# Scanning two states in one VectorE instruction, with a start column between them

## The chip, the cores and the metric

One core of a Trainium2 chip runs the whole program. The metric is the device time of one execution in microseconds; the time given for a kernel is the median of several runs. A profile is one further execution, recorded instruction by instruction; its span is the time from the first to the last instruction.

## The reference

Two sequences of 2048 tokens with 256 channels are normalised (layer norm) to `xn`. The result is `x + scan(xn) + experts(xn)`.

The scan part sorts the tokens of each sequence by their nearest of eight means, and runs a selective scan along the sorted order, with 16 states for each channel:

```
delta = softplus(dt_proj(u) + bias)                    # per token and channel
h[n]  = exp(delta * A[n]) * h[n] + (delta * u) * B[n]  # for each of 16 states n
y     = sum over n of h[n] * C[n]  +  D * u
```

The rows `y` are then put back into the tokens' own order. The expert part is a mixture of eight experts (two linear maps up to 512 with a SiLU gate, one down to 256), of which each token takes the best two.

## The kernel before

**Stages.** A front part of some 110 us normalises, scores, sorts and routes the tokens. After it, the scan and the experts run interleaved to the end. The scan is cut into 8 pieces of 512 positions (`CH`), four for each sequence; channels lie on the 128 partitions, in two halves `h`. The expert work is cut into 71 tiles of 128 tokens, each made of two parts up (8 matmuls each as written, which the trace records as 16) and one part down.

**The scan of a piece.** `gather` fetches the rows, `turn` transposes them to `u`, `project` makes delta, B and C, `step_size` and `series` make `dl` (delta, with softplus as a series of squares by ScalarE and multiply-adds by VectorE) and `du` (delta * u). `load_b` brings B of four states, repeated on all partitions, into a tile `bt`; `load_z` and `mask_z` bring C into a block form `z`. Then come steps (`Step`), one for a group `q` of four states and a half `h`: 64 in all. In a step, for each state `i`:

- `decay(i)`: ScalarE computes `da = exp(dl * A)`, 512 columns;
- `feed(i)`: VectorE computes `bu = du * bt[i]`;
- `scan(i)`: VectorE scans `da` and `bu` along the 512 positions, starting from a column of `carry` (or from 0 in a sequence's first piece), and writes every fourth element of `hs`, so that the four states of a position lie together.

`keep_last` copies the last position to `carry` (ScalarE). `turn(i)` (in `Step`) transposes four blocks of `hs` on TensorE into a PSUM tile `pt_s` (two buffers), which ScalarE copies to `ht`; `contract(i)` multiplies `ht` with `z` and sums the states in PSUM (`ys`). At a piece's end `take_sums` copies the sums to `yt` and `add_sums` adds its rows, through GpSimd, to `acc` or, for the last piece, to the output.

**The order.** The order of instructions on each engine is that of the program's text, so the loop at its end decides it. It counts in places: each step has `NSUB` = 4 places, and in place `i` of step `k` it emits the next product, `scan(i)`, `decay(i)` of the step after, and part of the transposes and contractions of the step before (places 1 and 2 turn, place 3 contracts). `at_place(step, place, ...)` puts all other scan work (loads, masks, series, projections, sums) at chosen places. The experts' parts (`jobs`) are given out at a pace: as many as keep the planned TensorE time in a fixed ratio to the planned VectorE time (`on_pe`, `on_dve`); those still left 16 scans before the end are all emitted there. VectorE's work on a part (`silu`, `gate`) is emitted two places after the part's matmuls (`later`). Once all experts' parts are out, the two halves of `acc` are copied to the output, and the last piece's rows are added to that.

**Queues.** `load_b`, `load_z` and the store of the projection go through SP's queue in the order of the text, each waiting there until its tile is free; weight tiles, token rows and row additions go through GpSimd's.

**Buffers.** `bt` two tiles of four states, `da` six tiles of one state, `bu` three, `hs` three tiles of four states, `ht` four, `pt_s` two.

## Time and profile before

| | before |
|---|---|
| median of 3 runs | 800.16 us (799.86 to 808.87) |
| the profiled execution | 793.45 us |
| its span | 791.7 us |
| TensorE busy | 712.9 us (90%) |
| VectorE busy | 711.3 us (90%) |
| ScalarE busy | 507.9 us (64%) |
| GpSimd busy | 520.9 us (66%) |
| mean granted TensorE clock | 0.951 |

How to read it: the shares are of the whole span, and so mix the front part, the interleaved part and the end. The chain of work that ended last runs over TensorE for 69% of the span and over VectorE for 3%. Lines of groups give the line, the engine, the operation, what is written and read, the shapes and the number of instructions, then busy us and mean ns of one, then the idle time just ahead of them. DMA lines give the number of issues, KB each, and the median time from issue to landing. Numbers of lines are those of the kernel before.

### The profile page before, as it was taken

To read this page: it belongs to the slowest core of one execution; us is meant where nothing else is said; L and a number is where in the kernel's file an instruction comes from. 1 tells how busy PE (TensorE), PEld (TensorE's weight loads), DVE (VectorE), ACT (ScalarE), POOL (GpSimd) and SP (SyncE) were. 2 spreads that over 40 slices of the span, in tenths; PEclk is the share of its full clock that TensorE was granted. 3 is DMA by queue.
4 is the path that set the end of the run, shared out by engine and by line. 5 is a ranking of instruction groups with operands and counts; after the bars stand their busy time and mean duration, and the time that the engine had idled before them with its cause. 6 is when DMAs were issued, how large, how long until landed. Compare 5 with 4: busy or idle time off the path is not lost.

```text
span 791.7 us, 16967 instructions
## 1 busy us (share of the span) xinstructions
PE 712.9 (90%) x6552; PEld 605.5 (76%) x6552; DVE 711.3 (90%) x1162; ACT 507.9 (64%) x986; POOL 520.9 (66%) x374
## 2 busy tenths in 40 slices
PE   7385979899999999899999999999999998999963
PEld 5144768589877988599868986798779885998842
DVE  8865269899999999899989999899999998899991
ACT  4821266586669657776668666866687576757572
POOL 2023738657867886788776787878678787686313
PEclk9755999999999999999999999999999998999996
DMA  8593244664368547855656367448644855444462
GB/s 280 222 323 114 58 173 108 210 172 97 108 155 244 154 106 215 203 148 143 206 140 176 56 247 219 107 95 263 197 111 132 273 156 112 107 102 96 86 219 27
DMA packets 61215, 125.90 MB, mean 159 GB/s; under 512 B 24464, under 2 KB 42032, under 8 KB 53776
## 3 DMA queue, kind: packets, MB, share of 16 engines
q0 software_dynamic: 40224, 65.03, 34.6%
q1 hardware_dynamic: 20912, 59.80, 22.1%
q8 instruction: 52, 0.85, 0.4%
q14 instruction: 27, 0.22, 0.1%
HBM read 180.06 MB, written 27.00 MB: 262 GB/s over the span
## 4 chain that ended last, share of the span: by engine, by line
PE 69%; ACT 6%; DVE 3%; issue 3%; DMA 2%; POOL 1%; POOLq 0%; SPq 0%; ACTq 0%; DVEq 0%
PE p_ps L875 28%; PE py L898 14%; PE pt_s L787 12%; PE y L796 6%; ACT ht L791 2%; DMA out_dram<-acc 2%; PE y L728 2%; PE pt_g L858 2%; PE px L655 2%; PE pd L692 1%; DVE hs L775 1%; ACT da L760 1%; DVE bu L766 1%; PE px L660 1%; PE pt_u L641 1%
## 5 line engine op out<-in xcount | busy, mean ns | idle before, releaser
L875 PE MATMUL p_ps<-xT,w 128*128 128x128 f32 x2272 | 280.3, 279 | 5.3 <-ACT sq L702 4.3
L875 PEld LDWEIGHTS p_ps<-xT,w 128*128 128x128 f32 x2272 | 268.2, 195 | 20.2 <-issue 9.3
L775 DVE TENSOR_TENSOR_SCAN hs<-da,carry,bu 128x512 f32<-128x512 f32 x192 | 246.2, 1283 | 0.0
L760 ACT ACTIVATE da<-dl,na 128x512 f32<-128x512 f32 x256 | 182.0, 723 | 1.1 <-DVE hs L775 1.0
L816 POOL DMA_INDIRECT acc<-yo,token_of x71 | 137.8, 1941 | 60.3 <-ACT yo L902 20.0
L766 DVE TENSOR_TENSOR bu<-du,bt 128x512 f32<-128x512 f32 x256 | 174.0, 680 | 0.0
L791 ACT COPY ht<-pt_s 128x512 f32<-128x512 f32 x256 | 137.1, 590 | 31.3 <-PE pt_s L787 31.0
L787 PE MATMUL pt_s<-ident,hs 128*128 128x128 f32 x1024 | 137.9, 279 | 14.7 <-ACT ht L791 8.7
L835 POOL DMA_INDIRECT w<-in_w_up_dram,w_row x71 | 94.8, 1335 | 84.2 <-DVE w_row L584 36.8
L898 PE MATMUL py<-w,g 128*128 128x256 f32 x568 | 139.0, 389 | 12.2 <-ACT r L696 8.7
L787 PEld LDWEIGHTS pt_s<-ident,hs 128*128 128x128 f32 x1024 | 117.7, 143 | 31.6 <-ACT ht L791 15.6
L898 PEld LDWEIGHTS py<-w,g 128*128 128x128 f32 x568 | 104.2, 193 | 27.1 <-ACT r L696 10.3
L849 POOL DMA_INDIRECT xg_sb<-xn,token_of x71 | 88.3, 1243 | 37.5 <-issue 30.2
L835 POOL DMA_INDIRECT w<-in_w_down_dram,w_row x71 | 93.5, 1317 | 21.6 <-issue 12.5
L883 ACT ACTIVATE t_sb<-p_ps 128x512 f32<-128x512 f32 x71 | 42.5, 599 | 69.4 <-PE p_ps L875 69.1
L902 ACT ACTIVATE yo<-py,own 128x256 f32<-128x256 f32 x71 | 33.8, 476 | 80.5 <-PE py L898 80.3
L775 DVE TENSOR_TENSOR_SCAN hs<-da,bu 128x512 f32<-128x512 f32 x64 | 78.2, 1223 | 0.0
L796 PE MATMUL y<-ht,z 128*32 128x128 f32 x2048 | 74.3, 279 | 2.5 <-ACT ht L791 1.9
L816 POOL DMA_INDIRECT acc<-yt,line_of x28 | 54.7, 1952 | 25.7 <-ACT ht L791 8.2
L796 PEld LDWEIGHTS y<-ht,z 128*32 128x32 f32 x2048 | 51.1, 110 | 24.5 <-issue 13.2
L888 DVE SCALAR_TENSOR_TENSOR t_sb<-t_sb,p_ps 128x512 f32<-128x512 f32 x71 | 48.2, 679 | 9.1 <-ACT t_sb L883 8.8
L892 DVE SCALAR_TENSOR_TENSOR g<-t_sb,p_ps 128x512 f32<-128x512 f32 x71 | 48.3, 681 | 7.2 <-PE p_ps L875 4.7
(188 smaller groups left out, 632.8 us busy)
## 6 DMA issues: line engine op xcount, KB each, us to landing
bt<-bc SPq DMA_DIRECT2D x32, 1024.0 KB, 5.4
z<-bc SPq DMA_DIRECT2D x32, 256.0 KB, 3.8
xn<-xt SPq DMA_DIRECT2D x8, 520.0 KB, 2.6
xt<-in_x_dram SPq DMA_DIRECT2D x8, 512.0 KB, 7.5
acc<-in_x_dram SPq DMA_DIRECT2D x8, 512.0 KB, 6.4
w<-in_w_up_dram,w_row POOLq DMA_INDIRECT x71
w<-in_w_down_dram,w_row POOLq DMA_INDIRECT x71
xg_sb<-xn,token_of POOLq DMA_INDIRECT x71
```

The source lines that it names most:

```text
L760: nc.scalar.activation(self.da[i], self.piece.dl[:, self.h, :], AF.Exp, scale=na[:, self.h, n : n + 1])
L766: nc.vector.tensor_mul(self.bu[i], self.piece.du[:, self.h, :], self.piece.bts[self.q][:, i, :])
L775: nc.vector.tensor_tensor_scan(self.hs[:, :, i], self.da[i], self.bu[i], start, ALU.mult, ALU.add)
L787: nc.tensor.transpose(pt[:, j, :], self.hs[:, t0 : t0 + G, :].rearrange("p t n -> p (t n)"), ident)
L791: nc.scalar.copy(self.ht[i], pt)
L796: nc.tensor.matmul(p.ys[self.h][j * G : (j + 1) * G, i, :], lhsT=p.zs[q][:, i * (P // G) + j, :], rhs=self.ht[i][:, j, :], start=False, st ...
L816: ins = nc.gpsimd.indirect_dma_start(out=to, out_offset=bass.IndirectOffsetOnAxis(ap=numbers, axis=0), in_=rows, in_offset=None, compute_o ...
L835: nc.gpsimd.indirect_dma_start(out=to[self.t % NW], out_offset=None, in_=rows, in_offset=bass.IndirectOffsetOnAxis(ap=w_row[:, self.t : se ...
L849: nc.gpsimd.indirect_dma_start(out=self.xg, out_offset=None, in_=xn_d, in_offset=bass.IndirectOffsetOnAxis(ap=token_of[:, self.t : self.t ...
L875: nc.tensor.matmul(p[:, f, :], lhsT=wk[:, h, f * P : (f + 1) * P], rhs=self.xT[:, h, :], start=h == 0, stop=h == ND - 1,)
L892: nc.vector.scalar_tensor_tensor(self.g, self.s, 0.5, self.p3, ALU.mult, ALU.mult)
L898: nc.tensor.matmul(py, lhsT=self.g[:, f, :], rhs=w2[:, f, :], start=f == 0, stop=f == NH - 1)
```

## The change

Two states of a half are now scanned by one VectorE instruction of 1026 columns: 513 for each state. The first column of each state has a decay of 0 and an input that is the state to begin from, so the running value is replaced there. A step covers eight states: four pairs `o`, each made of states `o` and `o + 4` of the eight.

- `bt` becomes `[P, 2, 2, 513]`: it holds two pairs. Each `load_b` issues two DMAs, each for two rows of B that go behind their start columns. A new `begin(i)` lets ScalarE copy four carried states (or zeros) into the start columns of one `bt` tile.
- `du` gets a start column of 1.0 (a memset for each piece), so that the product puts the carried state into `bu`.
- `da` becomes three lasting tiles of two states, with start columns set to 0 once. `decay` still computes one state at a time.
- `feed` and `scan` work on pairs, four of each in a step; the scan starts from 0.0 in all pieces. `hs` has two tiles of eight states.
- A step has eight places: scans in even ones, products in odd ones. Transposes stand in places 1, 2, 4 and 5 of the following step, contractions in 3 and 6.
- `load_b`, `load_z`, `mask_z`, `begin` of the sums, `take_sums` and `add_sums` get other places, in units of four as before. The planned VectorE times are 2.1 and 1.1 us for the two kinds of place.

```diff
         def load_b(self, q: int):
-            bt = scn.tile([P, Q, CH], F32, tag="b", name="bt")
-            nc.sync.dma_start(
-                bt, bc_d[self.b][self.c][q * Q : (q + 1) * Q, :].partition_broadcast(P)
-            )
+            bt = scn.tile([P, 2, 2, CH1], F32, tag="b", name="bt")
+            r0 = q // 2 * 2 * Q + q % 2 * 2
+            for o in range(2):
+                rows = bc_d[self.b][self.c][r0 + o : r0 + o + Q + 1 : Q, :]
+                nc.sync.dma_start(bt[:, o, :, 1:], rows.partition_broadcast(P))
             self.bts[q] = bt
...
-                self.du = prep.tile([P, ND, CH], F32, tag="du", name="du")
+                self.du = prep.tile([P, ND, CH1], F32, tag="du", name="du")
+                nc.vector.memset(self.du[:, :, 0:1], 1.0)
...
+        def begin(self, i: int):
+            p = self.piece
+            nc.scalar.copy(
+                p.bts[2 * self.s + i][:, :, :, 0],
+                carry[:, self.s, self.h, 2 * i : 2 * i + 2, :] if p.c
+                else zero[:, 0:4].rearrange("p (o n) -> p o n", n=2),
+            )
...
-            nc.scalar.activation(
-                self.da[i], self.piece.dl[:, self.h, :], AF.Exp, scale=na[:, self.h, n : n + 1]
-            )
+            nc.scalar.activation(
+                self.da[o][:, n, 1:], self.piece.dl[:, self.h, :], AF.Exp,
+                scale=na[:, self.h, state : state + 1],
+            )
...
+        def feed(self, o: int):
+            self.bu[o] = scn.tile([P, 2, CH1], F32, tag="bu", name="bu", bufs=2)
             nc.vector.tensor_mul(
-                self.bu[i], self.piece.du[:, self.h, :], self.piece.bts[self.q][:, i, :]
+                self.bu[o], self.piece.du[:, self.h, :].unsqueeze(1).to_broadcast([P, 2, CH1]),
+                self.piece.bts[2 * self.s + o // 2][:, o % 2],
             )
...
-                self.hs = late.tile([P, CH, Q], F32, tag="hs", name="hs", bufs=3)
-            start = carry[:, q, h, i : i + 1] if p.c else 0.0
+                self.hs = late.tile([P, 2, CH1, Q], F32, tag="hs", name="hs", bufs=2)
             nc.vector.tensor_tensor_scan(
-                self.hs[:, :, i], self.da[i], self.bu[i], start, ALU.mult, ALU.add
+                self.hs.rearrange("p n t o -> p (n t) o")[:, :, o],
+                self.da[o].rearrange("p n t -> p (n t)"), self.bu[o].rearrange("p n t -> p (n t)"),
+                0.0, ALU.mult, ALU.add,
             )
...
-            at_place(max(s0 + 2 * q - 3, 0), NSUB - 1 if n or q > 1 else 0, lambda p=p, q=q: p.load_b(q))
+        for q, place in ((1, -2), (2, 10), (3, 14)):
+            if n or q > 1:
+                at_place(s0 - 1, NSUB + place, lambda p=p, q=q: p.load_b(q))
...
+        if step:
+            if i % 2 == 0:
+                step.scan(i // 2)
+            elif i // 2 + 1 < Q:
+                step.feed(i // 2 + 1)
+            elif after_:
+                after_.feed(0)
+            if i == 1:
+                step.begin(1)
+            if after_ and i == 5:
+                after_.begin(0)
+            if i + AHEAD < N_STEP:
+                step.decay(i + AHEAD)
+            elif after_:
+                after_.decay(i + AHEAD - N_STEP)
+        if before_:
+            if i == 0:
+                before_.keep_last()
+            elif i in (1, 2, 4, 5):
+                for j in range(2):
+                    before_.turn(i // 4, (i - 1) % 3 * 2 + j)
+            elif i in (3, 6):
+                before_.contract(i // 4)
```

In the piece's count of 32 places, the loads of `bt` for groups 0 to 3 now stand at places -6, -2, 10 and 14 relative to the piece's first scan; `begin` of these tiles for the first half stands at -3, 1, 13 and 17, and the first products from them at -1, 3, 15 and 19.

## The prediction

> **What bounds the kernel now.** I read four views in this order: busy time by stretch, the waits inside the scan loop, the groups of instructions, and the timeline of the last scans. The first says which engines are full. Its columns are the stretch (start:end in us), its length, then busy us and instructions of TensorE, weight load, VectorE, ScalarE and GpSimd, the granted clock, the DMA share and GB/s.
>
> ```profile
> 115.00:200.00 85.00, 80.57 (x731) 70.00 (x731) 81.65 (x133) 55.03 (x110) 58.94 (x42) 1.00 0.50 138
> 200.00:280.00 80.00, 78.42 (x767) 67.42 (x766) 77.98 (x112) 57.56 (x114) 61.73 (x40) 1.00 0.60 164
> 280.00:360.00 80.00, 76.09 (x719) 66.47 (x718) 76.20 (x111) 56.13 (x111) 62.83 (x42) 0.98 0.62 166
> ...
> 746.00:780.00 34.00, 24.15 (x291) 17.37 (x290) 29.63 (x33) 22.19 (x40) 4.05 (x2) 0.90 0.51 159
> ```
>
> From 115 to 746 us TensorE is busy 609.8 of 631 us and VectorE 607.1: idle 21.2 and 23.9 us. Two engines are full at once. From 746 us, when the expert work is over, only VectorE is. Is a "full" TensorE really full? In the timeline around 322 us a run of sixteen p_ps matmuls starts at 321.79 and the next block at 323.57: 111 ns each, and the blocks behind it follow at the same rate without a gap. It works at its own pace; it isn't waiting for data while shown as busy.
>
> Next, who holds whom in that loop (TensorE's waits from 115 to 746 us, us in total, times, longest):
>
> ```profile
> PE py L898 <- ACT r L696: 7.7, 4, 3.1
> PE pt_s L787 <- ACT ht L791: 5.8, 9, 0.9
> ...
> PE p_ps L875 <- DVE g L892: 0.4, 1, 0.4
> ```
>
> TensorE's idle time hangs on ScalarE, which itself waits there almost only for TensorE; VectorE releases 0.4 us of it. The 7.7 us are two pauses of 3.1 us (at 328 and 665 us) and little else: py waits for one of the two buffers of its PSUM pool, which pd holds until ScalarE has made e and r from it behind a decay, a square and a carry; the matmuls right after the pause run at half speed (8 of py in 3.4 us instead of 1.9). So the change takes work from an engine that is full, beside another that is as full and hardly waits for it.
>
> **The change, part by part.** *VectorE's instructions.* Scans go from 256 of 512 columns to 128 of 1026, products likewise. The rows:
>
> ```profile
> L775 DVE TENSOR_TENSOR_SCAN hs<-da,carry,bu 128x512 f32<-128x512 f32 x192 | 246.2, 1283 | 0.0
> L766 DVE TENSOR_TENSOR bu<-du,bt 128x512 f32<-128x512 f32 x256 | 174.0, 680 | 0.0
> L775 DVE TENSOR_TENSOR_SCAN hs<-da,bu 128x512 f32<-128x512 f32 x64 | 78.2, 1223 | 0.0
> ...
> L538 DVE TENSOR_TENSOR_SCAN cum<-keep,both 128x256 f32<-128x256 f32 x1 | 0.7, 693 | 0.0
> ...
> L301 DVE TENSOR_TENSOR fm_c<-sc,bm 128x256 f32<-128x256 f32 x1 | 0.4, 424 | 0.0
> ```
>
> A scan costs (1223 - 693)/256 = 2.07 ns a column, so 1026 columns without a start from a tile cost 1223 + 514 x 2.07 = 2287 ns. A product costs (680 - 424)/256 = 1.0 ns a column: 680 + 514 = 1194 ns. Reading du twice through a stride of 0 is free by a near row: the product with mask, also stretched by such a stride, takes 672 ns for 512 columns. Durations may not simply be added up, as the timeline of the last scans shows:
>
> ```profile
> 760.73 1.28 DVE L775 TENSOR_TENSOR_SCAN hs<-da,carry,bu 128x512 f32<-128x512 f32 x1
> ...
> 761.92 0.67 DVE L766 TENSOR_TENSOR bu<-du,bt 128x512 f32<-128x512 f32 x1
> ...
> 762.51 1.28 DVE L775 TENSOR_TENSOR_SCAN hs<-da,carry,bu 128x512 f32<-128x512 f32 x1
> ```
>
> A scan and a product of 1.95 us together come round every 1.78: each starts 0.09 us before the one ahead ends. Two states cost 3.57 us now (3.45 without a carried start, 60 ns less each), and 2.287 + 1.194 - 0.18 = 3.30 after. The saving is 96 x 0.27 + 32 x 0.15 = 30 us, not the 53 us that the durations alone would give. Eight memsets take back under 1. VectorE in the loop: 607 to about 578 us, 92%.
>
> A rule speaks against this. The Trainium skill (Vector Engine (DVE) Microarchitecture Reference, Measured stream behaviour on trn2) says that pairs of words beginning at an odd word cost 1.30 ns a column on both sources where even ones cost 1.054. With 513 words a row, every second row begins at an odd word; no row of this trace does. By the rule a product could cost up to 1026 x 0.25 = 0.25 us more, 32 us in all, and the saving is gone; by the rows it costs nothing. I take the rows (a long row has one odd start, the rule's case has one at each pair) and keep the rule for a rival.
>
> *ScalarE.* 64 new copies into the column between the states, 24 copies of carry less (48 to 24), at 180 ns (carry copy in the timeline): +7.2 us on 458 of 665; ScalarE idles 172 us of the loop, so the work itself is hidden. Where the cover fails is the wait below.
>
> *A new wait on ScalarE.* Begin writes into bt and must wait until bt has landed; until now only the product on VectorE did. In the new order a load of bt waits for the product in place 9 of a piece's 32 (one place: a scan or a product), SP issues it, ScalarE reaches begin in place 13, and the product needs it in place 15. The other three loads have the same spacing; before, a load came eight places ahead. Behind begin in ScalarE's queue stand a decay, the copies ht of the same place and the experts' copies, and TensorE waits for these. Places last (775.6 - 117.1)/256 = 2.57 us, so the lead to begin is 3.5 x 2.57 = 9.0 us. What does a load take?
>
> ```profile
> bt<-bc SPq DMA_DIRECT2D x32, 1024.0 KB, 5.4
> z<-bc SPq DMA_DIRECT2D x32, 256.0 KB, 3.8
> ...
> bc<-xd SPq DMA_DIRECT2D x8, 64.0 KB, 2.2
> ```
>
> From below: 5.4 us as now, plus 0.33 for a second issue, 5.7. But rows of a partition no longer lie side by side, so pieces shrink from 8 KB to 2 KB. Of such pieces z is made: 3.8 - 2.2 = 1.6 us for 256 KB beyond the smallest transfer, hence 2.2 + 4 x 1.6 = 8.6 us for 1 MB, 8.9 with the issue. z's spread is 2.9 to 7.9 us, bt's 4.3 to 9.6. I take 7 us, between the two, as the queues' own mean (22.1% of 16 x 791.7 us over 20,912 packets, 134 ns each of 2.9 KB) makes 32 packets an engine 4.3 us or less. It fits the lead by 2 us in the median; a late quarter of the 32 loads, some 2 us over and half of that hidden by the two buffers of pt_s, costs about 2 us in all, at worst as in the slower rival. The queue order bears it: SP has the store of xd in front of one load a piece (place 12 before 14), and the loads of z wait for contractions only one place earlier (19 for 20, 22 for 23), with three places and more to the next bt.
>
> *Tiles.* hs has two buffers of eight states instead of three of four. VectorE may write the first buffer again in place 16, TensorE has turned it in place 13, so VectorE can be two to three places ahead; the experts' silu, put two places behind its matmuls, already holds it there. da is six states in both. Costed at 0 with that cover, up to 3 us a step without it. TensorE gets states three places after their last scan, before two: nothing lost.
>
> *TensorE.* Same transposes, contractions and experts: 609.8 us stay.
>
> *Head and tail.* First scan: one wide product instead of a narrow one, +0.5 us. After the last expert's gate 16 scans are left, as before: 8 x 3.30 = 26.4 against 16 x 1.78 = 28.5 us, -2.1. But what follows the last scan doubles: four turns took from 775.8 to 779.0 us, eight take 2.8 us more and a contraction half a microsecond: +3.3. The copy of acc to the output ended at 771.5 and is not what the end waits for. Tail +1.2.
>
> *Sum.* Of TensorE's 21.2 us idle, 6.2 are the two pauses and stay, as step_size keeps its places; of the other 15, held by ScalarE, I let a quarter go because ScalarE's decays and VectorE's gates come earlier: -4. With +2 for late loads, +0.5 and +1.2: about 0, between -4 and +4. Against its own execution of 793.45 us (span 791.7 and 1.75 around it) that is 793 us. The median of the runs, 800.16, lies 0.8% above; scaled, 800 us. As late loads may stay away I say 798.
>
> **The rivals.**
>
> *A. TensorE stays full (forecast).* For: 97% busy, 0.4 us released by VectorE. Against: two engines at 97% cost each other something that no wait names. 792 to 808 us.
>
> *B. The coupling was the price: faster.* With VectorE at 92% TensorE loses nearly all of its 15 us, and the tail gives 2: -17 us, 2.1%, 783 us. For: VectorE idles only 23.9 us, mostly behind ScalarE's squares. Against: the waits.
>
> *C. ScalarE stands before bt: slower.* Loads of 2 KB pieces beside the experts' weights (DMA share 0.6) take z's price and z's doubling, 9 to 16 us, against a lead of 9. It decides from a landing of about 10.5 us, where the two buffers of pt_s no longer hide it. At a mean of 12 us, 3 late and 1 to 1.5 of it seen by TensorE, 32 loads cost 32 to 48 us: 832 to 848; at 10.5 to 11, 816 to 825. For: lead cut to three and a half places. Against: a 1 MB load lands in 5.4 us now.
>
> *D. VectorE does not get quicker.* Odd rows cost the rule's 0.25 us: no saving, tail +3.3 and head +0.5 remain: 803 us, up to 818 if TensorE now waits for scans.
>
> **How the numbers follow.** A 0.40, B 0.15, C 0.35, D 0.10 (0.07 within 2%, 0.03 above). Faster by over 2% 0.15, within 2% 0.47, slower by over 2% 0.38; 2% is about what a measurement of this kernel can tell from no change. The time is A's, 798, with its own range of 788 to 808. The full range cuts B's better half and C's worse third: 783 to 832 us.
>
> **What would show it.** Right: scan rows of 2.29 us and product rows of 1.19, VectorE near 578 us of the loop while TensorE is still at 97%; bt landing in 6 to 8 us; no wait of bt's copy for a DMA over 1 us. Product rows above 1.35 mean D. Waits of bt on ScalarE for bt's DMA, then TensorE on ht, mean C. TensorE idle below 10 us in the loop means B. The forecast is wrong if TensorE's busy time in the loop changes, or if the loop itself is over 12 us longer or shorter.

## The result and the profile after

The changed kernel takes **854.58 us** (median of four runs, 851.05 to 860.40) against 804.28 us for the kernel before (four runs): a ratio of **1.063**, with a 95% interval of 1.053 to 1.073. It is slower by 6%, and lies above the forecast of 798 us and above the whole range of 783 to 832 us. The kernel before was measured anew beside every group of runs below, with medians from 794.86 to 805.5 us; so ratios are compared, not times.

First the groups of the page of the changed kernel: engine totals, then line, engine, operation, shapes, count, busy us and mean ns of one, and the idle time just ahead with what ended most of it.

```profile
PE 732.9 (85%) x6552; PEld 613.6 (71%) x6552; DVE 694.7 (81%) x917; ACT 511.9 (60%) x1026; POOL 577.8 (67%) x374
...
L795 DVE TENSOR_TENSOR_SCAN hs<-da,bu 128x1026 f32<-128x1026 f32 x128 | 293.8, 2295 | 11.9 <-ACT da L780 5.2
...
L787 DVE TENSOR_TENSOR bu<-du,bt 128x1026 f32<-128x1026 f32 x128 | 156.2, 1220 | 19.3 <-ACT bt L767 18.8
...
L860 POOL DMA_INDIRECT w<-in_w_up_dram,w_row x71 | 99.6, 1403 | 80.3 <-DVE w_row L586 36.9
...
L860 POOL DMA_INDIRECT w<-in_w_down_dram,w_row x71 | 115.2, 1622 | 21.6 <-issue 13.7
```

The two instructions of the change last what the prediction gave them (2295 against 2287 ns, 1220 against 1194). VectorE has less to do, 694.7 us instead of 711.3. But look at GpSimd (POOL), which has not one instruction more and was left out of the prediction: 577.8 us instead of 520.9. Its issues of the experts' weights have grown. These are the same rows in the page of the kernel before:

```profile
L835 POOL DMA_INDIRECT w<-in_w_up_dram,w_row x71 | 94.8, 1335 | 84.2 <-DVE w_row L584 36.8
...
L835 POOL DMA_INDIRECT w<-in_w_down_dram,w_row x71 | 93.5, 1317 | 21.6 <-issue 12.5
```

Next the changed kernel's busy time by stretch, with the columns of the table shown in the prediction:

```profile
200.00:280.00 80.00, 74.77 (x718) 63.85 (x720) 72.49 (x77) 54.13 (x112) 61.53 (x37) 1.00 0.62 154
280.00:360.00 80.00, 73.44 (x686) 61.58 (x678) 70.86 (x78) 53.54 (x110) 61.81 (x37) 1.00 0.60 153
...
440.00:520.00 80.00, 68.01 (x642) 59.98 (x640) 65.77 (x74) 48.33 (x98) 63.90 (x39) 0.98 0.53 130
```

Between 200 and 280 us TensorE was busy 78.42 us and VectorE 77.98; now 74.77 and 72.49, with 718 matmul instructions done instead of 767. Both engines that were full have holes, everywhere in the loop. From the first scan to the last expert matmul the loop took 634.1 us before (117.06 to 751.1) and takes 688.7 now (123.51 to 812.2): +54.6 of the +66.8 us of span. The rest is +5.7 behind the last expert matmul and +6.4 ahead of the first scan. The last is not the change's own: the front part is the same, and in other profiles of changed versions the first scan stands anywhere from 115.55 to 123.52 us. The trace of the changed kernel is of the longest of its four executions (860.40 us), and that of the kernel before is of a short one (793.45 us); so these differences are somewhat larger than the 50.3 us between the two medians.

What ended the idle time in the loop (engine, line, what it waited for: us in total, times, longest), 115 to 812 us:

```profile
DVE t_sb L913 <- ACT t_sb L908: 22.9, 19, 5.2
...
DVE bu L787 <- ACT bt L767: 18.8, 9, 8.4
PE pt_s L811 <- ACT ht L815: 18.2, 20, 2.2
...
PE py L923 <- DMA w<-in_w_down_dram,w_row: 13.5, 6, 7.5
```

Two waits of TensorE are new in size: that for `ht` (5.8 us before), and that for the down weights, which the list of before doesn't have. From the first scan to the last expert matmul TensorE idles 63.6 us instead of 21.4. VectorE's wait for `begin` is the one that the prediction feared. Is it because `bt` lands late? No: among ScalarE's waits in this stretch there is none for the DMA of `bt`. The longest of these pauses shows what it hangs on. This is GpSimd's part of the changed kernel's timeline (start, duration, engine, line; in brackets the idle time ahead and what ended it):

```profile
500.43 1.86 POOL L622 DMA_INDIRECT xs<-xn,line_of  x1 [0.30 <-issue]
502.60 1.85 POOL L622 DMA_INDIRECT xs<-xn,line_of  x1 [0.30 <-issue]
504.75 0.95 POOL L622 DMA_INDIRECT xs<-xn,line_of  x1 [0.30 <-issue]
506.00 1.83 POOL L622 DMA_INDIRECT xs<-xn,line_of  x1 [0.30 <-issue]
508.14 1.46 POOL L874 DMA_INDIRECT xg_sb<-xn,token_of  x1 [0.30 <-issue]
509.90 2.73 POOL L841 DMA_INDIRECT acc<-yo,token_of  x1 [0.30 <-ACT da L780]
512.93 1.78 POOL L860 DMA_INDIRECT w<-in_w_down_dram,w_row  x1 [0.30 <-issue]
515.02 2.39 POOL L860 DMA_INDIRECT w<-in_w_up_dram,w_row  x1 [0.31 <-DMA acc<-yo,token_of]
```

And the other engines in the same stretch:

```profile
514.33 2.29 DVE L795 TENSOR_TENSOR_SCAN hs<-da,bu 128x1026 f32<-128x1026 f32 x1
...
522.04 3.33 PE L923 MATMUL py<-w,g 128*128 128x256 f32 x7 [7.53 <-DMA w<-in_w_down_dram,w_row]
...
525.83 0.47 ACT L927 ACTIVATE yo<-py,own 128x256 f32<-128x256 f32 x1 [10.91 <-PE py L923]
526.20 0.19 ACT L767 COPY bt<-zero 128x4 f32<-128x4 f32 x1
...
526.42 1.23 DVE L787 TENSOR_TENSOR bu<-du,bt 128x1026 f32<-128x1026 f32 x1 [8.42 <-ACT bt L767]
```

Read it upwards from the last line. VectorE waits 8.42 us for `begin`. `begin` stands in ScalarE's queue behind `yo`, which waits 10.91 us for `py`. TensorE waits 7.53 us for down weights. They are those issued at 512.93 (the issue ahead of that one stands at 496.96, and the one after it ends 0.1 us before the matmul). It comes at the end of a line of issues with only the queue's own 0.30 us between them: GpSimd is behind with its work.

A long pause of TensorE can cost more than its length. This is the stretch from the end of the pause, with the columns of the table above:

```profile
520.00:526.50 6.50, 4.46 (x13) 3.67 (x14) 0.08 (x1) 0.67 (x3) 3.59 (x4) 0.50 0.96 355
```

The granted clock is 0.50 there, and the seven matmuls of `py` in the line above take 3.33 us. In the loop of the changed kernel the trace has six such stretches of 3.4 or 6.8 us, 30.7 us in all; the kernel before has two, 10.2 us. TensorE's busy time in the loop is 625.1 us instead of 612.6, for much the same matmuls; at half clock the 20.5 us more would account for some 10 of these 12.5 us (an estimate).

And single issues of GpSimd differ: the same `xs` issue takes 0.95 us or 1.85; the `w_up` issue beside the 2.29 us scan takes 2.39 and ends 0.8 us after it.

Sorting GpSimd's issues in the loop by what VectorE runs when they start gives the rule of this trace. In the changed kernel the median `w_up` issue takes 0.99 us (9 cases) beside an idle VectorE and 2.38 us (16 cases) when it starts beside a scan; in the kernel before, where a scan lasts 1.2 to 1.3 us, 0.99 (5) and 1.49 (23). `xg` takes 0.97 (10) and 2.17 us (15), before 0.97 (5) and 1.43 (19). The ends are sharper than the medians: from the first scan on, all 68 issues of weights and `xg` that start beside a scan in the changed kernel end 0.75 to 0.88 us after the end of that scan. (In the kernel before 65 of 79 do; the others start within the first 0.06 or the last 0.15 us of a scan.) It is not a matter of VectorE being busy, as `silu` and `gate` show, of whose two inputs one lies in PSUM (`p_ps`):

```profile
321.81 0.69 DVE L913 SCALAR_TENSOR_TENSOR t_sb<-t_sb,p_ps 128x512 f32<-128x512 f32 x1 [0.69 <-ACT t_sb L908]
...
322.31 1.00 POOL L860 DMA_INDIRECT w<-in_w_up_dram,w_row  x1 [0.30 <-PE pt_s L811]
```

The 37 issues that start beside one of these take 0.97 to 1.07 us, as beside an idle VectorE. So **an issue that starts beside a scan is held until the scan ends, and scans have become twice as long.** The Trainium skill (GPSIMD Engine Reference, 1. Specifications) names a contention that fits: GpSimd shares its SBUF interfaces with VectorE and contends with VectorE instructions that have two SBUF inputs, which scans and products are. It doesn't say that DMA issues are held, nor for how long; these rows do.

Do the transfers themselves take longer as well? For those of GpSimd's queue, no. Its packets took 31.8% of the changed span of 858.5 us and 34.6% of 791.7 us before, which is 273 and 274 us for each of the 16 DMA engines:

```profile
q0 software_dynamic: 40224, 65.03, 31.8%
...
q0 software_dynamic: 40224, 65.03, 34.6%
```

### The profile page after: what moved, and what is told of

It reads as the page before. It is cut to its first block, busy times and chain, and to the rows that moved or that the text cites. A ratio compares the mean times of both kernels' runs of the same rounds, so it can differ in the third digit from the quotient of the medians.

```text
span 858.5 us, 16877 instructions
## 1 busy us (share of the span) xinstructions
PE 732.9 (85%) x6552; PEld 613.6 (71%) x6552; DVE 694.7 (81%) x917; ACT 511.9 (60%) x1026; POOL 577.8 (67%) x374
## 3 DMA queue, kind: packets, MB, share of 16 engines
q0 software_dynamic: 40224, 65.03, 31.8%
## 5 line engine op out<-in xcount | busy, mean ns | idle before, releaser
L795 DVE TENSOR_TENSOR_SCAN hs<-da,bu 128x1026 f32<-128x1026 f32 x128 | 293.8, 2295 | 11.9 <-ACT da L780 5.2
L841 POOL DMA_INDIRECT acc<-yo,token_of x71 | 143.6, 2022 | 77.1 <-ACT yo L927 13.8
L787 DVE TENSOR_TENSOR bu<-du,bt 128x1026 f32<-128x1026 f32 x128 | 156.2, 1220 | 19.3 <-ACT bt L767 18.8
L923 PE MATMUL py<-w,g 128*128 128x256 f32 x568 | 145.8, 402 | 27.2 <-DMA w<-in_w_down_dram,w_row 13.5
L860 POOL DMA_INDIRECT w<-in_w_up_dram,w_row x71 | 99.6, 1403 | 80.3 <-DVE w_row L586 36.9
L923 PEld LDWEIGHTS py<-w,g 128*128 128x128 f32 x568 | 108.1, 201 | 44.7 <-ACT r L700 12.2
L860 POOL DMA_INDIRECT w<-in_w_down_dram,w_row x71 | 115.2, 1622 | 21.6 <-issue 13.7
L874 POOL DMA_INDIRECT xg_sb<-xn,token_of x71 | 98.2, 1383 | 37.3 <-DVE tot L462 16.0
L841 POOL DMA_INDIRECT acc<-yt,line_of x28 | 61.9, 2209 | 29.9 <-ACT ht L815 13.8
L885 ACT COPY xT<-pt_g 128x256 f32<-128x256 f32 x71 | 26.9, 378 | 51.9 <-PE pt_g L883 40.1
```

The lines of the kernel that those rows point to most:

```text
L787: nc.vector.tensor_mul(self.bu[o], self.piece.du[:, self.h, :].unsqueeze(1).to_broadcast([P, 2, CH1]), self.piece.bts[2 * self.s + o // 2] ...
L795: nc.vector.tensor_tensor_scan(self.hs.rearrange("p n t o -> p (n t) o")[:, :, o], self.da[o].rearrange("p n t -> p (n t)"), self.bu[o].re ...
L841: ins = nc.gpsimd.indirect_dma_start(out=to, out_offset=bass.IndirectOffsetOnAxis(ap=numbers, axis=0), in_=rows, in_offset=None, compute_o ...
L860: nc.gpsimd.indirect_dma_start(out=to[self.t % NW], out_offset=None, in_=rows, in_offset=bass.IndirectOffsetOnAxis(ap=w_row[:, self.t : se ...
L874: nc.gpsimd.indirect_dma_start(out=self.xg, out_offset=None, in_=xn_d, in_offset=bass.IndirectOffsetOnAxis(ap=token_of[:, self.t : self.t ...
L923: nc.tensor.matmul(py, lhsT=self.g[:, f, :], rhs=w2[:, f, :], start=f == 0, stop=f == NH - 1)
```

## The experiments

Eighteen experiments follow; in two of them (e14, e17) an earlier kernel is measured again. They ask in turn about VectorE's missing saving, the shape of the DMAs, the width of the instructions, the wait behind `begin`, the tiles, the order of the transposes, and the end.

### VectorE's saving, the pieces and whole rows: e1 to e4

In the changed order a product stands directly ahead of the scan that reads it. e1 puts it one scan earlier. It has three `bu` tiles for that (and, for room, one `xd` and four `own`):

```diff
             if i % 2 == 0:
+                if i // 2 + 1 < Q:
+                    step.feed(i // 2 + 1)
+                elif after_:
+                    after_.feed(0)
                 step.scan(i // 2)
-            elif i // 2 + 1 < Q:
-                step.feed(i // 2 + 1)
-            elif after_:
-                after_.feed(0)
```

> The changed kernel with the product of a pair emitted ahead of the scan before it (three bu tiles instead of two; xd gets one tile and own four, to make room), so that no scan follows directly on the product it reads. Theory P (the product stands directly before its scan): in the last pairs of the changed kernel a pair takes 3.52 us, where 3.30 was expected and two old pairs took 3.57; here a pair takes 3.30 to 3.35 us, VectorE gets 128 x 0.2 = 25 us back and the kernel comes down by 12 to 25 us, to about 830-842. Theory D (pieces of 2 KB in the loads of bt slow all transfers): pair 3.3 us but time within 5 us of the changed kernel, about 850-855. Theory S (the coarser steps and tighter buffers stretch the loop): likewise 0 to 8 us.

Measured: ratio 1.0725 (1.0661 to 1.079). The waits of e1, where the scan's row now has no idle time ahead of it at all:

```profile
DVE bu L787 <- ACT bt L767: 94.1, 48, 7.5
```

The product, emitted earlier, meets `begin` before ScalarE has reached it, 48 times. The gap between product and scan was real: in e1 a scan starts 0.08 us before the end of the product ahead of it (the median of 127), which it no longer reads. But closing the gap in this way buys a larger wait. The one earlier place that was tried is early enough for the scan and too early for `begin`.

e2 makes pairs of neighbouring states and keeps B's rows in DRAM with a spare word, so that one DMA brings whole rows of a half tile, where the change has two DMAs of 2 KB pieces:

```diff
-            r0 = q // 2 * 2 * Q + q % 2 * 2
-            for o in range(2):
-                rows = bc_d[self.b][self.c][r0 + o : r0 + o + Q + 1 : Q, :]
-                nc.sync.dma_start(bt[:, o, :, 1:], rows.partition_broadcast(P))
+            rows = bc_d[self.b][self.c][q * Q : (q + 1) * Q, :]
+            nc.sync.dma_start(
+                bt.rearrange("p o n t -> p (o n) t"), rows.partition_broadcast(P)
+            )
...
-            state = self.s * S8 + n * Q + o
+            state = self.s * S8 + 2 * o + n
```

> The changed kernel with neighbouring states as pairs and with rows of 513 words in DRAM, so that one DMA of whole rows (8.2 KB pieces) fills a bt tile, instead of two DMAs in 2 KB pieces; z is then made of every second row, in 2 KB pieces as before. Theory D: about 12,300 fewer packets, GpSimd's transfers of weights fall back from 1622 and 1403 ns to about 1320 and 1335, ScalarE waits less for bt, and the kernel comes down by 25 us or more, to 825 or less. Theory P: no change over 5 us (850-855). Theory S: no more than 8 us.

Measured: 1.0527 (1.0475 to 1.058). That is a point below the changed kernel's 1.063, but the two intervals overlap, so a gain isn't shown. Together with e1's edit (e3, with three `own` tiles):

> Both edits together in the changed kernel (products ahead, whole rows; own three tiles). P and D both true: the sum of the two gains, 800 to 820. If S holds most of the loss: still above 835 with a pair at 3.3 us and weights at 1320 ns.

Measured: 1.0656 (1.0624 to 1.0688), with `bu` waiting 82.6 us for `begin` again. And the pieces put alone into the kernel before, its `bt` rows 513 words long and fetched by two DMAs:

```diff
-            bt = scn.tile([P, Q, CH], F32, tag="b", name="bt")
-            nc.sync.dma_start(
-                bt, bc_d[self.b][self.c][q * Q : (q + 1) * Q, :].partition_broadcast(P)
-            )
+            bt = scn.tile([P, Q, CH + 1], F32, tag="b", name="bt")
+            for o in range(2):
+                rows = bc_d[self.b][self.c][q * Q + 2 * o : q * Q + 2 * o + 2, :]
+                nc.sync.dma_start(bt[:, 2 * o : 2 * o + 2, 1:], rows.partition_broadcast(P))
```

> The kernel before, in which only bt changes: four rows of 513 words, filled by two DMAs in 2 KB pieces behind a spare word, read from the second word on. Theory D: GpSimd's transfers get longer and the kernel slower by 15 us or more (815 to 835). Theories P and S: within 5 us of before (800-806), as bt is loaded eight places ahead there and products and scans are as before. The products read from an odd word: a row above 0.69 us would show a price of that.

Measured: 1.002 (1.0002 to 1.0038). The smaller pieces cost 0.2% where the rest of the kernel is in balance. So if the point in e2 is real, it is not a price of the pieces as such; in e11 below the same edit makes a version slower by a point.

### The width: e5 to e9

e5 leaves all of the change in place (order, tiles of eight, start columns, `begin`) and only cuts each wide instruction in two of 513 columns:

```diff
-            nc.vector.tensor_tensor_scan(
-                self.hs.rearrange("p n t o -> p (n t) o")[:, :, o],
-                self.da[o].rearrange("p n t -> p (n t)"), self.bu[o].rearrange("p n t -> p (n t)"),
-                0.0, ALU.mult, ALU.add,
-            )
+            for n in range(2):
+                nc.vector.tensor_tensor_scan(
+                    self.hs[:, n, :, o], self.da[o][:, n], self.bu[o][:, n], 0.0, ALU.mult, ALU.add,
+                )
```

and the product likewise.

> The changed kernel with its tiles, order, places, buffers and loads, but each wide product and each wide scan made by two instructions of 513 columns. Theory W (wide VectorE instructions hold GpSimd's DMA issues for longer: an issue beginning beside a scan took a median of 1.87 to 3.1 us after and 1.4 to 2.3 before, one beside no VectorE work about 1.0 in both, so weights and rows come late): issues fall back to the lengths of before (weights about 1.33 us) and the kernel comes down by 30 us or more, to 825 or below, although VectorE has 25 us more to do. Theory O (the order in steps of eight, the begin copies and the tighter buffers): it stays at 850 or gets slower by up to 20 us. The second halves read da, bu and bt from an odd word: over 0.1 us more than the first halves would be the price of that.

Measured: 1.0362 (1.0334 to 1.0391). From the page of e5:

```profile
L797 DVE TENSOR_TENSOR_SCAN hs<-da,bu 128x513 f32<-128x513 f32 x256 | 299.8, 1215 | 0.0
...
L788 DVE TENSOR_TENSOR bu<-du,bt 128x513 f32<-128x513 f32 x256 | 165.0, 688 | 12.7 <-ACT bt L767 12.7
...
L860 POOL DMA_INDIRECT w<-in_w_up_dram,w_row x71 | 89.5, 1260 | 89.1 <-DVE w_row L586 36.2
```

VectorE has *more* to do (703.3 us busy) and the kernel is about 2.7 points faster (the changed kernel's ratio is itself uncertain by a point): what the change was made of, the wide instruction, is a main part of what costs. GpSimd's time falls to 528.2 us, and the `w_up` issue from 1403 to 1260 ns. The products of 513 words, every second of which begins at an odd word, take 688 ns, against 680 for 512.

e6 gives `begin` to VectorE, so that nothing of ScalarE stands ahead of the product:

```diff
-            nc.scalar.copy(
+            nc.vector.tensor_copy(
                 p.bts[2 * self.s + i][:, :, :, 0],
```

> The changed kernel with the copies into bt's start columns on VectorE instead of ScalarE, at the same places of the text. Theory B (ScalarE's begin couples the two engines: VectorE waited 18.8 us for it, and 94 us where products stood ahead of scans): 64 small copies of 0.2 us cost VectorE 13 us, the wait for ScalarE goes, and the kernel gets 10 us or more faster, 840 or less. Theories W and O without B: 0 to 10 us slower, 850 to 865.

Measured: 1.071 (1.0689 to 1.073). The wait for `begin` is gone from the list and nothing is gained: VectorE then waits for other things (its wait for ScalarE's `t_sb` is 28.6 us). So that wait was not what the kernel lost by; in the timeline above it hung on a pause of TensorE.

e7 is the kernel before with two `hs` tiles instead of three:

```diff
-                self.hs = late.tile([P, CH, Q], F32, tag="hs", name="hs", bufs=3)
+                self.hs = late.tile([P, CH, Q], F32, tag="hs", name="hs", bufs=2)
```

> The kernel before with two tiles hs instead of three: VectorE may write a tile again two places after TensorE has turned it, where the change leaves about three. Theory H (the tighter hs is a main cause): 15 us or more slower than before, 810 or more. Theories W, B and D: within 4 us of before.

Measured: 0.9998 (0.9985 to 1.0012). Nothing, in that kernel.

e8 is the changed kernel without the experts' weight loads behind the first three tiles:

```diff
-            if i == 1 and t + NW < NT:
-                tiles[t + NW].load_up()
...
-            if t + NW < NT:
-                tiles[t + NW].load_down()
```

> The changed kernel that leaves out the loading of expert weights after the first three tiles (later tiles multiply with those): GpSimd issues half as many transfers and some 54 MB less are moved; TensorE, ScalarE and VectorE do the same work. Theory W and theory D (loads late through GpSimd or the DMA engines): 35 us or more faster, 820 or less. Theory O or B: within 15 us of the changed kernel.

Measured: 1.0362 (1.0337 to 1.0386), the same as e5, although the instructions are wide. Two different ways of having GpSimd's transfers in time, narrow instructions or no weight loads, bring about the same. This run answers a rival too: wide instructions could also cost because VectorE's small work for the experts has to wait behind them. They are wide here, and of TensorE's waits in the loop this is the largest for that work:

```profile
PE p_ps L900 <- DVE t_sb L913: 2.3, 2, 1.9
```

But loads also cost traffic; would the kernel before gain as well without them? e15, the same edit in the kernel before:

> The kernel before without the experts' weight loads after the first three tiles (later tiles compute with old weights). Theory (its weights are not late): 0.99 to 1.00, so that the 2.7 points which the changed kernel gained without them were the price of their lateness. Rival (the weights' traffic and GpSimd's time for it cost every version): 0.96 to 0.98.

Measured: 1.0034 (1.0018 to 1.005). It gains nothing. So the 2.7 points are the price of *late* transfers, and only the changed kernel pays it. The weights are the larger part of them; without their loads GpSimd is also in time with the rows `xs`, for which TensorE waited 5.8 us in the changed kernel and not at all in e8.

e9, and e14 which is the same kernel measured again, put width alone into the order of before: steps of four states, products and scans of two states, no start columns:

```diff
-                self.bu[i], self.piece.du[:, self.h, :], self.piece.bts[self.q][:, i, :]
+                self.bu[i // 2], self.piece.du[:, self.h, :].unsqueeze(1).to_broadcast([P, 2, CH]),
+                self.piece.bts[self.q][:, i : i + 2, :],
...
-                if i + 1 < NSUB:
-                    step.feed(i + 1)
-                elif k + 1 < len(steps):
-                    steps[k + 1].feed(0)
-                step.scan(i)
+                if i == 0:
+                    step.feed(2)
+                elif i == 2 and k + 1 < len(steps):
+                    steps[k + 1].feed(0)
+                if i % 2 == 0:
+                    step.scan(i)
```

> The kernel before, in its own order, steps, loads and carried starts, with two tiles hs, in which one product and one scan of 1024 columns take the place of two each (128 of each); the second state of a pair runs on from the first one's last value and the states of hs stand in another arrangement, so that part of the computation is left out. TensorE's order is that of before. Theory W (wide VectorE instructions cost more through GpSimd and through waiting than they save): 15 to 35 us slower than before, 810 to 830, with GpSimd's weight issues at 1.4 to 1.6 us. Theory O (the order in steps of eight is the loss): VectorE saves 20 us or more and the kernel is as before or up to 10 us faster, 785 to 796.

> The kernel before with two hs tiles and with products and scans of 1024 columns, in its own order; the start of the second state and the arrangement of the results are left out; measured again for a narrower interval. Theory (a wide instruction holds GpSimd's issues, and this costs of itself): 1.01 to 1.03. Rival (it costs only in an order that already makes TensorE wait): 0.99 to 1.00.

Measured: e9 1.0123 (1.0039 to 1.0207, too wide to tell), e14 **1.0228** (1.0187 to 1.027). From the page of e14:

```profile
L777 DVE TENSOR_TENSOR_SCAN hs<-da,carry,bu 128x1024 f32<-128x1024 f32 x96 | 225.1, 2345 | 1.5 <-ACT da L761 1.2
L839 POOL DMA_INDIRECT w<-in_w_up_dram,w_row x71 | 107.7, 1517 | 77.3 <-DVE w_row L584 36.6
...
L839 POOL DMA_INDIRECT w<-in_w_down_dram,w_row x71 | 108.7, 1531 | 21.6 <-issue 14.9
```

In the order of before, with no new order of transposes, no `begin` and no pieces, halving the number of VectorE's instructions takes 19 us off VectorE's busy time (692.5 us), adds 57 to GpSimd's (578.2), and makes the kernel 2.3% slower. TensorE's largest wait there is for the rows `xs` that GpSimd fetches:

```profile
PE pt_u L641 <- DMA xs<-xn,line_of: 9.8, 5, 3.7
```

With 1.6 us for down weights that is 11.4 of the 15.0 us which TensorE idles more in the loop than before. GpSimd's issues are held in the same way: all 69 that start beside a scan end 0.75 to 0.88 us after it. Whether all of the 2.3% comes through GpSimd isn't shown.

### The order of the transposes: e10 to e13, e16, e17

The changed order emits transposes in the adjoining places 1, 2 and 4, 5. In the program of TensorE this makes 23 runs of 16 transposes with nothing between, where before there were 13: the second eight then wait until ScalarE has emptied a buffer of `pt_s`. e10 is e5 with the transposes at places 1, 3, 4, 6 (6 such runs are left):

```diff
-            elif i in (1, 2, 4, 5):
-                for j in range(2):
-                    before_.turn(i // 4, (i - 1) % 3 * 2 + j)
-            elif i in (3, 6):
-                before_.contract(i // 4)
+            if i in (4, 7):
+                before_.contract(i // 5)
+            if i in (1, 3, 4, 6):
+                for j in range(2):
+                    before_.turn(i // 4, (0, 2)[i in (3, 6)] + j)
```

with the planned TensorE times moved along.

> The kernel of e5 (split instructions) with the transposes in places 1, 3, 4 and 6 and the contractions in 4 and 7, so that runs of 16 transposes, in which TensorE waits for ScalarE to empty one of two PSUM tiles, become 6 instead of 23 (before: 13). Theory O: TensorE's wait for ht falls from 18 to under 8 us and the kernel by 8 to 15 us, to 810-817. If order hardly matters: within 4 us of e5 (825).

Measured: 1.0162 (1.0072 to 1.0252), and again as e17:

> The version with narrow instructions and moved transposes, measured again for a narrower interval. Theory (moving the transposes is worth about two points once the instructions are narrow, and late weights are hardly left): 1.006 to 1.016, next to the 1.006 without weight loads. Rival (weights still late by a point or more): 1.016 to 1.025.

Measured: 1.0143 (1.0057 to 1.0229). Two points less than e5. The wait of `pt_s` for `ht` has nearly gone (first e5, then e17):

```profile
PE pt_s L811 <- ACT ht L815: 21.8, 24, 2.2
...
PE pt_s L811 <- ACT ht L815: 2.8, 5, 1.0
```

e11 is e5 with e2's whole rows, e12 has the moved transposes as well:

> e5 and e2 together: split instructions and bt loaded by one DMA of whole rows. If D's part (ratio 1.063 to 1.053 in e2) is its own cause: 815 to 819. If it was a part of W's (late transfers): 822 to 826, as e5.

> e5, e2 and the transposes of e10 together. If the three causes are all of the loss but the longer end (5 us): 798 to 808. If something else of the order is left: above 812.

Measured: 1.0481 (1.0399 to 1.0563) and 1.0162 (1.0081 to 1.0243). Whole rows make the narrow version a point slower than e5, clear of the intervals; in the wide version they seemed a point faster, and with transposes moved they change nothing. No fixed price of the pieces fits this; why e11 is slower was not looked into.

Do width and order add up? e13 moves the transposes in the changed kernel itself, with its wide instructions:

> The changed kernel, wide instructions kept, with only the transposes of a step moved to places 1, 3, 4, 6 and the contractions to 4, 7. Theory (width and order add): it gains the two points that the same move brought the version with split instructions, from 1.063 to about 1.043, and the runs of sixteen transposes in front of a wait for ht go. Rival 1 (the late weights decide, and the order is hidden behind them): 1.055 to 1.065. Rival 2 (the order is nearly all): below 1.03.

Measured: 1.0636 (1.06 to 1.0671). The time is that of the changed kernel, within its interval of a point to either side, as the first rival said. TensorE's waits in e13:

```profile
PE py L923 <- DMA w<-in_w_down_dram,w_row: 16.0, 9, 3.4
...
PE y L821 <- ACT ht L815: 4.6, 13, 0.9
PE p_ps L900 <- DMA w<-in_w_up_dram,w_row: 3.9, 5, 2.0
```

The wait of `pt_s` for `ht` falls to 1.8 us, and the waits for weights grow: 16.0 us for down weights in nine pauses instead of six, and up weights too. But they take back only a part of it. From the first scan to the last expert matmul e13 takes 673.2 us, 15.5 less than the changed kernel, and TensorE idles 47.0 us in it instead of 63.6. So the first rival's mechanism, an order hidden behind late weights, is not what the trace shows. The end, on the other hand, is longer, 52.2 us instead of 46.3, because GpSimd waits there for the copy of `acc`, while the sums are ready 5.8 us ahead of the first addition (1.4 in the changed kernel):

```profile
823.80 0.58 ACT L742 COPY yt<-y 128x512 f32<-128x512 f32 x1 [0.55 <-PE y L821]
...
830.20 1.54 POOL L841 DMA_INDIRECT out_dram<-yt,line_of  x1 [19.31 <-DMA out_dram<-acc]
```

These are single traces from two groups of runs, and two traces of one kernel differ by 1.3 us (e9 and e14) and 6.7 us (e10 and e17) in the same stretch. How many of the 15.5 us belong to the order, and whether the longer end is all that hides them in the time, isn't settled.

e16 is e10 (narrow, transposes moved) without the weight loads behind the first three tiles.

> The changed kernel with each wide product and scan as two of 513 columns and the transposes moved, and without the experts' weight loads after the first three tiles (later tiles compute with old weights). Theory (the weights are in time once the instructions are narrow, what remains is the tail and the order): within half a point of the version with the loads, 1.01 to 1.016. Rival (late weights still hold it): 0.99 to 1.00.

Measured: 1.006 (1.0038 to 1.0083). That lies between the two expectations. From the first scan to the last expert matmul its profile has 633.0 us, the kernel before 634.1: the loop is whole again, and what remains is the end (49.1 us). Between 1.0143 and 1.006 the intervals overlap; whether some lateness of weights is left in e10 and e17 isn't settled. The ratios together:

| | transposes as in the change | transposes moved |
|---|---|---|
| wide, with weight loads | 1.063 | 1.064 |
| narrow, with weight loads | 1.036 | 1.016 and 1.014 |
| wide, without loads | 1.036 | not run |
| narrow, without loads | not run | 1.006 |

### The end: e18

In the trace of the changed kernel the row additions of the seventh piece stand at 804.5 to 813 us on GpSimd, eight us ahead of the last expert matmul's end (before: at 724.9 to 733, with 18 us to spare). The last experts' additions queue behind them, and SP issues the copy of `acc` to the output at 831.54, 19 us behind that matmul instead of 5.5. These are the last scan, its first transposes, the last contraction and the first addition to the output in the changed kernel:

```profile
834.16 2.30 DVE L795 TENSOR_TENSOR_SCAN hs<-da,bu 128x1026 f32<-128x1026 f32 x1
...
836.61 3.79 PE L811 MATMUL pt_s<-ident,hs 128*128 128x128 f32 x16 [4.88 <-DVE hs L795]
...
843.98 1.23 PE L821 MATMUL y<-ht,z 128*32 128x128 f32 x32
...
847.26 1.54 POOL L841 DMA_INDIRECT out_dram<-yt,line_of  x1 [18.82 <-DMA out_dram<-acc]
```

GpSimd waits for the copy, not for the sums. e18 leaves the seventh piece's additions out:

```diff
-        at_place(s2 + 1, 3, lambda p=p, to=to: p.add_sums(to))
+        if n != 6:
+            at_place(s2 + 1, 3, lambda p=p, to=to: p.add_sums(to))
```

> The changed kernel, with the rows of the seventh of its eight pieces not added to acc at all (that part of the result is missing). Theory (these four additions, now at the end of the expert work, push the last experts' additions and with them the copy of acc to the output behind the last piece's sums): the time from the last expert matmul to the end falls from 46.3 us to 42 to 44, the ratio from 1.063 to about 1.06. Rival (the end waits for the last piece's sums alone): 46 us stay.

Measured: 44.9 us from the last expert matmul to the end, against 46.3 in the changed kernel and 40.6 before; ratio 1.0671 (1.0592 to 1.0751), the same within its interval. The output now waits for the sums (`yt`). So the copy was worth some 1.4 us, and most of the 5.7 is the doubled work behind the last scan: from its end to the span's end 20.7 us in e18, 16.1 before. Both were at work, and neither of the two expectations was right by itself.

## Why the prediction was wrong, step by step

Two steps failed. The prediction put nothing down for GpSimd, whose DMA issues are held by the longer scans; and it said of the transposes "nothing lost", though their new order makes TensorE wait for `ht`. Here is each step in turn.

**What bounds the kernel: half right.** TensorE and VectorE were both full, and VectorE was not what TensorE waited for: e14, with 19 us less of work on it, is slower. But the step went from "these two engines are full" to "only these two matter". GpSimd had 62 of 80 us in the same table, and the prediction never asked what a longer VectorE instruction does to it. This is the missing term. Width costs 2.3% in the order of before (e14) and about 2.7 points in the changed one (e5, e8).

**VectorE's 30 us: durations right, saving wrong.** 2295 and 1220 ns were measured. The step "minus 0.18" failed: it carried over an overlap of 0.09 us at both seams. The timeline of the last scans of the changed kernel:

```profile
827.12 2.30 DVE L795 TENSOR_TENSOR_SCAN hs<-da,bu 128x1026 f32<-128x1026 f32 x1
829.34 1.20 DVE L787 TENSOR_TENSOR bu<-du,bt 128x1026 f32<-128x1026 f32 x1
830.64 2.30 DVE L795 TENSOR_TENSOR_SCAN hs<-da,bu 128x1026 f32<-128x1026 f32 x1
```

The product starts 0.08 us before the scan ahead of it ends, as predicted. But the scan at 830.64 starts 0.10 *after* its product's end (829.34 + 1.20 = 830.54), because it reads what that product writes; before, the product directly ahead of a scan was another state's. A pair takes 3.52 us where 3.30 were predicted and 3.57 were taken before: 0.05 saved instead of 0.27. Over 128 pairs 0.22 us too little makes some 28 us, nearly the whole saving. It did not decide the result, since VectorE was not the bound; e1, which closes the gap, is no faster.

**The odd-word rule: rightly put aside.** It asked for up to 250 ns more in a product of 1026 columns; 26 more than worked out were measured, and 688 ns for one of 513 columns against 680 for 512. In e5 every second product begins at an odd word, and both kinds have a median of 689 ns.

**ScalarE and the new wait: right in the term that was argued, beside the point in effect.** (Its 172 us of idle time are 631 less the 458 of a longer stretch; from 115 to 746 us ScalarE is busy 436.1, so it idles 195. The argument stays as it is.) The load of `bt` is in time: ScalarE never waits for it in the loop. VectorE does wait for `begin`, 18.8 us, since `begin` stands behind copies that wait for TensorE. With `begin` on VectorE (e6) nothing is gained. Rival C's range was the nearest of all, but its mechanism did not occur; the nearness is luck.

**Tiles: 0, unrefuted.** Two `hs` tiles cost nothing in the kernel before (e7); for the changed one it wasn't isolated.

**"TensorE: same transposes, 609.8 us stay": wrong.** The number of matmuls stayed, their order did not. "TensorE gets states three places after their last scan: nothing lost" looked at when states are ready, and not at what stands between two groups of eight transposes, which share two buffers. Moving them is worth two points with narrow instructions (e5 to e10 and e17), where the wait for `ht` falls by 19.0 us. With wide ones (e13) the loop gets shorter too, but the whole time does not. The busy time did not stay either: 625.1 us instead of 612.6, with the granted clock at 0.50 for longer.

**Head and tail: +1.2 predicted, +5.7 measured for the tail.** From the last expert matmul to the end of the last scan it is 24.3 us against 24.5: 0.2 us saved, not 2.1 (the seam again). The doubled work behind the last scan costs 4.6 us (e18), not 3.3. Its first 16 transposes meet a clock of 0.50: they take 3.79 us in the changed kernel, where two runs of eight took 1.07 and 1.15 us before, at a clock of 1.00 (first the changed kernel's stretch, then three lines of the kernel before):

```profile
834.00:840.50 6.50, 3.89 (x20) 3.18 (x24) 2.36 (x2) 1.77 (x4) 0.00 (x0) 0.50 0.93 323
...
775.50:779.40 3.90, 3.33 (x48) 2.45 (x48) 0.13 (x1) 2.22 (x5) 0.00 (x0) 1.00 0.02 4
...
775.78 1.07 PE L787 MATMUL pt_s<-ident,hs 128*128 128x128 f32 x8 [0.86 <-DVE hs L775]
...
777.14 1.15 PE L787 MATMUL pt_s<-ident,hs 128*128 128x128 f32 x8 [0.29 <-ACT ht L791]
```

And "the copy of acc is not what the end waits for" became false, for 1.4 us.

**The sum.** It was a balance of small terms that did exist, around 0. The two terms that made most of the 6%, width through GpSimd (about 2.7 points) and the order of the transposes (2), were not in it, and no rival held them: A, B and D priced VectorE and TensorE, C priced a DMA on SP. With both undone 1.4 points are left (e17); the longer end is a part of them, and the rest was not taken apart.

## What to carry to other kernels

Ahead of merging instructions with two SBUF inputs on VectorE into longer ones, look at what GpSimd issues in the same stretch: in the trace of the changed kernel 79 of the 80 issues of weights and gathered rows that started beside a scan were held to its end, so fewer and longer instructions can cost more than their fixed parts save, even where neither engine looks like the bound. Where an edit measures zero, look at the stages before calling it worth nothing: e13's loop is shorter and its end longer. And test a second cause also with the first removed (e5, then e10). When a step doubles in size, ask not only when its data are ready but what its instructions now stand next to: product beside its scan, transposes beside transposes.

## What the runs showed of the hardware

- GpSimd's indirect DMA issue takes 0.97 to 1.0 us beside an idle VectorE (`w_up`, `xg`) and 2.2 to 2.4 us in the median when it starts beside a scan of 2.3 us; with scans of 1.2 to 1.3 us it is 1.4 to 1.5. Each of the 68 issues of weights and `xg` that start beside a scan of the changed kernel ends 0.75 to 0.88 us after the scan; beside VectorE instructions with an input in PSUM the issue takes 0.97 to 1.07 us (37 cases).
- Two VectorE instructions back to back overlap by 0.08 to 0.09 us if the second doesn't read what the first writes; if it does, it starts 0.10 to 0.11 us behind the end. The difference of 0.19 us is most of the 0.27 that merging was to save for a pair.
- The granted clock of TensorE is 0.50 in 30.7 us of the changed kernel's loop and in 10.2 us of that before, each time in or right behind a pause of TensorE; the stretches last 3.4 or 6.8 us.
- A start from a tile costs a scan about 60 ns (1283 against 1223 ns for 512 columns, and 2345 against 2283 for 1024), at both lengths.
